# Turning layer 1's projection weights on VectorE instead of TensorE, and the masks of the first three steps on ScalarE

## The chip, the cores and the metric

The kernel runs on one core of a Trainium2 chip. The metric is device time in microseconds for one execution of the whole program; lower is better. The median of three runs before the change is 3088.62 us (3087.75 to 3088.84). Times "at" a point count from the start of the profiled span. Engines are PE (TensorE), DVE (VectorE), ACT (ScalarE), POOL (GpSimd) and SP, which only issues DMAs here; ACT issues DMAs too.

## The reference

64 graphs of 256 nodes with 512 features go through two attention layers. Layer 0 has 4 heads of 64, layer 1 has 8. All is float32.

```python
# layer 0
h = relu(layernorm(x))
q, k, v = h @ Wq, h @ Wk, h @ Wv                    # 512 -> 256
attn = softmax(where(adj, q k^T / 8, -max))
x = x + (attn v) @ Wo + bo
# layer 1
h = relu(layernorm(x))
h = layernorm(h) * gamma + beta
q, k, v = split(h @ w_qkv.T)                        # w_qkv is (1536, 512)
attn = softmax(where(adj | eye, q k^T / 8, -1e9))
x = x + (attn v) @ w_out.T + b_out                  # w_out is (512, 512)
```

Layer 1's weights come as (output, input). A matmul on PE contracts over the partitions, so the input feature has to lie on partitions: these weights have to be turned once.

## The kernel before

The work goes in 32 steps of two graphs each (512 tokens). In a step, tokens are split in 4 tiles of 128; the 512 features are split in 4 chunks (`c`) of 128 partitions. Everything is unrolled; nothing loops on the chip.

Each projection is done as a Strassen-like scheme of seven products (`PRODUCT`, `weight_sum`, `act_sums0`, `act_sums1`): a weight tile has 7 blocks, of which 4 are loaded; four sums (`weight_sum`, L404) make the other 3 and rewrite one of the 4, once. The activation tile `hT` has 7 blocks too, of which 4 are written from PSUM or placed by ACT, and four sums are made on POOL in every step (lines 407 to 412). A set of seven products for q and k is 28 matmuls (L841); the values of layer 0 use L888 in the turned form and L871 in the first two steps, those of layer 1 L922; the output projection L938, or L964 by rows in the first step. `evacuate` (L775 to L787) takes a product out of PSUM: products 1 and 2 by ACT copies, the others by DVE additions. Products 2, 4 and 3 go to the PSUM bank that 1, 7 and 5 had used, so product 3 waits for the evacuation of 5, and 4 for that of 7. The order in a set is 1, 6, 5, 2, 7, 3, 4; product 6 reads the activation sum `b[4]`, the second of POOL's sums (L410).

Attention of two heads is a "unit": scores on PE (L994), the mask added on DVE (L1017), exponentials on ACT (L1022), sums over halves of the keys on POOL (`pd`, L1029), turned and reduced on DVE (L1035, L1042, L1095 to L1107), sent through DRAM (`line`) and read back as the inverse sums (L1123), with which POOL normalises the result (L1141). `qk` of layer 0 is multiplied by the neighbour flags on POOL (L851).

The order on PE, DVE, ACT and POOL is written out by hand: `at(period, place, fn)` puts every piece at a place on a line, the pieces are sorted by it, and each engine gets its instructions in that order. A period (`PERIOD`, 6.4 places) is one step; negative periods are the start-up. Each engine works its own queue in order. SP is not in the list of hand-ordered engines, so the order of its DMAs follows from the build.

For the start-up before the change:

- `weight_load(n)` (L455 to L463) loads 4 x 128 rows of `w_qkv` (n = 0, 1, 2 for q, k, v) or of `w_out` (n = 3), one DMA of 1 MB each, into a buffer `wr` that is borrowed from another tile.
- `weight_block(wr, n, c)` (L465 to L473) turns one feature chunk `c`: four PE transposes (L468) into a PSUM bank, then two copies into the weight tile (L473), both on ACT for most q, k and v blocks, one on DVE and one on ACT for the first and for w_out. There are 16 such blocks, put between PE's pieces of steps 0 and 1.
- `weight_sum` for layer 1: q's on DVE (L404), the others on POOL.
- `mask(s, n)` (L544 to L551) makes the additive mask of a step from the adjacency on POOL (L549), 128 x 1024: 0 where there is an edge, -1e30 else. `mask0` then multiplies by the flags (L602), `mask1` by a tile that clears the diagonal (L610).
- `norm1` (L662 to L673) takes statistics of x on DVE and writes `h` = Relu(x - mean) on ACT (L673); `norm1_rest` takes h's statistics.
- In steps 0, 1 and the last, h is turned by PE; in the others by DVE in 32 x 32 blocks (`turn_blocks`, L724) with 16 DMAs (`move_blocks`, L736) that put the blocks in place, and ACT writes `hT` (`place_h`, L747, L749).

Of the kernel before, what the change touches and what calls it, by code (L numbers as in the profile page):

```python
# [18 lines left out]
LIMIT = 1e20  # L19


@with_exitstack
# [293 lines left out]
def fast_path(  # L316
# [61 lines left out]
    nc.vector.memset(extremes, 0.0)  # L378
    mhalf = const.tile([P, NT], FP, name="mhalf")
    nc.gpsimd.memset(mhalf, -0.5)  # L380

# [7 lines left out]

    Q, NQ = 32, P // 32
    NB = 7
    MARK = 64.0
# [20 lines left out]
    H0, H1, HD = I0 // 2, I1 // 2, D // 2  # L415
# [10 lines left out]
    def first_weights():  # L426
        for i in range(2):
            for k, w in enumerate((wq, wk)):
                nc.sync.dma_start(
                    wqk0[:, 2 * i:2 * i + 2, :, k, :].rearrange("p j c o -> p (j c) o"),  # L430
                    w[:, i * H0:(i + 1) * H0].rearrange("(c p) o -> p c o", p=P),
                )
        for i in range(2):
            nc.sync.dma_start(
                wv0[:, 2 * i:2 * i + 2].rearrange("p j c o -> p (j c) o"),
                wv[:, i * P:(i + 1) * P].rearrange("(c p) o -> p c o", p=P),
            )
# [8 lines left out]
        nc.scalar.dma_start(gbr[:NC], gamma.rearrange("(c p) -> c p", p=P))  # L446
        nc.scalar.dma_start(gbr[NC:], beta.rearrange("(c p) -> c p", p=P))
        return gbr

    def gamma_beta(gbr):  # L450
# [3 lines left out]

    def weight_load(n):  # L455

        if n == 1:
            wr = io.tile([P, 4, D], FP, name="wr", tag="xt")
        else:
            wr = act.tile([P, 4, D], FP, name="wr", tag="v1")  # L460
        src, r0 = (w_qkv, 4 * n) if n < 3 else (w_out, 0)
        nc.sync.dma_start(wr, src[r0 * P:(r0 + 4) * P].rearrange("(r p) i -> p r i", p=P))
        return wr  # L463

    def weight_block(wr, n, c):  # L465
        pw = mm_tile([P, 4 * P])
        for r in range(4):
            nc.tensor.transpose(pw[:, r * P:(r + 1) * P], wr[:, r, c * P:(c + 1) * P], ident)  # L468
        for i in range(2):
            blk = A_OF[i, c // HC]  # L470
            dst = wqkv1[:, blk, c % HC, n, :] if n < 3 else wo1[:, blk, c % HC, :]
            copy = nc.vector.tensor_copy if i == 0 and (n > 2 or (n, c) == (0, 0)) else nc.scalar.copy
            copy(dst, pw[:, i * H1:(i + 1) * H1])  # L473


    S = [dict() for _ in range(NSTEP)]
# [66 lines left out]

    def mask(s, n):  # L544
        if s < 2:
            edges, one = flat.bitcast(BF).rearrange("p (k c i) -> p k c i", k=NIC, i=P), 1.0
        else:
            edges, one = both[:, 1].rearrange("p k i t -> p k t i"), 1.0 + MARK
        nc.gpsimd.tensor_scalar(  # L549
            n.rearrange("p k g (c i) -> p k (g c) i", i=P), edges, -one, BIG, op0=ALU.add, op1=ALU.mult  # L550
        )  # L551

    def neighbours(s, g):

# [40 lines left out]
    def mask0(s):  # L595
# [4 lines left out]
        for kc in range(NIC):  # L600
            v = n0[:, kc].rearrange("p g n -> p (g n)")
            nc.gpsimd.tensor_tensor(v, v, st["ne"], ALU.mult)  # L602

    def mask1(s):
        st = S[s]
        n1 = st["n1"] = act.tile([P, NIC, G, N], BF, name="n1", bufs=2)
        mask(s, n1)
# [56 lines left out]
    def norm1(s, k):  # L664
        st, x1, t = S[s], S[s]["xt"], NORM1[k]
        if k == 0:
            st["mv"] = stat.tile([P, NT, 3], FP, name="mv1", bufs=2)
            st["mean"] = stat.tile([P, NT, 2], FP, name="mg", bufs=2)
            st["h"] = act.tile([P, NT, D], FP, name="h", tag="h" if s == NSTEP - 1 else "turned")
        mv, h = st["mv"], st["h"]  # L670
        moments(mv, x1, t)
        nc.scalar.mul(mv[:, t, 2:3], mv[:, t, 0:1], -1.0)
        nc.scalar.activation(h[:, t, :], x1[:, t, :], AF.Relu, bias=mv[:, t, 2:3])  # L673

    def second_bias(s, t):
        x1 = S[s]["xt"]
# [474 lines left out]
    def at(period, place, fn, *args):  # L1151
        events.append((period * (PERIOD if period >= 0 else FIRST) + place, len(events), fn, args))
# [77 lines left out]
    p = NSTEP - 2  # L1230
# [15 lines left out]
    for s in range(NSTEP):  # L1246
# [34 lines left out]
            at(p, place, adjacency_turn, s, a)  # L1281
        at(p, (FIRST_Q0 + 0.3, 3.74, 1.9)[s] if s < 3 else 3.58, mask0, s)
        at(p, (FIRST_Q0 + 0.31, 4.153)[s] if s < 2 else 5.85, mask1, s)
        if s == 0:
            at(p, FIRST_C0, first_transposes)
        else:
            for c in range(NC):
                if by_tensor(s, 0):
                    at(p, 2.9292 + 0.0001 * c, transpose_h, s, 0, c)
                else:  # L1290
                    at(p, AT_Q0 - 0.001 + 0.0001 * c, place_h, s, 0, c)
# [156 lines left out]
```

## Time and profile before

| | |
|---|---|
| median of 3 runs | 3088.62 us |
| the profiled execution | 3089.27 us, of which the span is 3087.4 us |
| granted PE clock | 1.00 |
| PE busy | 3068.8 us, 99% |
| DVE busy | 2539.7 us, 82% |
| POOL busy | 2308.9 us, 75% |
| ACT busy | 1207.4 us, 39% |
| DMA | 251.22 MB, mean 81 GB/s |

A line of the page's groups or of a timeline names the source line, the engine, the operation and the tiles, out<-in, then the number of instructions. In a timeline the first column is the start, the second the length of the merged stretch, and a bracket gives the idle time just before it and what ended it. PE's float32 matmuls appear as two records each, so a set of 28 shows x56. Matmuls overlap, and the end of each is modelled, so starts are the better measure on PE.

### The profile page before, as it was taken

To read this page: it belongs to the slowest core of one execution; us is meant where nothing else is said; L and a number is where in the kernel's file an instruction comes from. 1 tells how busy PE (TensorE), PEld (TensorE's weight loads), DVE (VectorE), ACT (ScalarE), POOL (GpSimd) and SP (SyncE) were. 2 spreads that over 40 slices of the span, in tenths; PEclk is the share of its full clock that TensorE was granted. 3 is DMA by queue.
4 is the path that set the end of the run, shared out by engine and by line. 5 is a ranking of instruction groups with operands and counts; after the bars stand their busy time and mean duration, and the time that the engine had idled before them with its cause. 6 is when DMAs were issued, how large, how long until landed. Compare 5 with 4: busy or idle time off the path is not lost.

```text
span 3087.4 us, 55474 instructions
## 1 busy us (share of the span) xinstructions
PE 3068.8 (99%) x20122; PEld 2528.5 (82%) x20122; DVE 2539.7 (82%) x4754; ACT 1207.4 (39%) x2136; POOL 2308.9 (75%) x2128
## 2 busy tenths in 40 slices
PE   8999999999999999999999999999999999999998
PEld 6878888888888888888888888888888888888887
DVE  7878888888888888888888888888888888888766
ACT  4434343344434343443434333443434344343431
POOL 7877877787877778777777778787777877777753
PEclk9999999999999999999999999999999999999999
DMA  4133232332322322223323233232332222331311
GB/s 152 53 95 92 57 90 74 93 94 64 86 74 87 94 84 70 84 73 100 93 55 92 72 93 94 67 83 73 87 94 87 68 84 75 99 93 52 93 34 50
DMA packets 187591, 251.22 MB, mean 81 GB/s; under 512 B 58088, under 2 KB 78192, under 8 KB 187312
## 3 DMA queue, kind: packets, MB, share of 16 engines
q1 hardware_dynamic: 123776, 179.93, 20.4%
q10 hardware_dynamic: 63536, 67.68, 7.6%
q8 instruction: 162, 2.65, 0.4%
q14 instruction: 117, 0.96, 0.1%
HBM read 128.59 MB, written 34.34 MB: 53 GB/s over the span
## 4 chain that ended last, share of the span: by engine, by line
PE 97%; POOL 2%; DVE 1%; issue 0%; DMA 0%; ACT 0%; ACTq 0%; SPq 0%; POOLq 0%; DVEq 0%
PE mm L841 37%; PE mm L938 18%; PE mm L922 13%; PE sc L994 9%; PE sc L1065 6%; PE mm L888 6%; PE mm L1065 5%; PE mm L994 3%; PE mm L871 1%; PE mm L964 0%; POOL pd L1029 0%; PE mm L468 0%; PE mm L700 0%; POOL xt L809 0%; POOL wqk L677 0%
## 5 line engine op out<-in xcount | busy, mean ns | idle before, releaser
L841 PE MATMUL mm<-hT,wqkv 128*128 128x256 f32 x3584 | 789.1, 380 | 1.9 <-DVE qk L779 0.9
L841 PEld LDWEIGHTS mm<-hT,wqkv 128*128 128x128 f32 x3584 | 677.3, 190 | 105.6 <-issue 11.8
L1029 POOL TENSOR_TENSOR pd<-p 128x512 f32<-128x512 f32 x383 | 479.6, 1274 | 257.5 <-ACT p L1022 199.6
L938 PE MATMUL mm<-wo,oT 128*128 128x256 f32 x2632 | 578.5, 379 | 0.0
L938 PEld LDWEIGHTS mm<-wo,oT 128*128 128x128 f32 x2632 | 499.8, 190 | 68.9 <-issue 0.7
L1022 ACT ACTIVATE p<-p 128x512 f32<-128x512 f32 x766 | 440.7, 626 | 119.3 <-DVE p L1017 109.1
L1017 DVE TENSOR_TENSOR p<-sc,n 128x512 f32<-128x512 f32 x579 | 362.6, 681 | 113.8 <-PE sc L994 113.6
L841 PE MATMUL mm<-hT,wqk 128*128 128x256 f32 x1792 | 398.7, 382 | 0.2
L922 PE MATMUL mm<-wqkv,hT 128*128 128x256 f32 x1792 | 395.5, 381 | 0.4 <-ACT v L775 0.4
L841 PEld LDWEIGHTS mm<-hT,wqk 128*128 128x128 f32 x1792 | 338.3, 191 | 55.8 <-issue 10.3
L922 PEld LDWEIGHTS mm<-wqkv,hT 128*128 128x128 f32 x1792 | 337.8, 190 | 55.7 <-issue 10.3
L809 POOL TENSOR_TENSOR xt<-xt,u 128x512 f32<-128x512 f32 x183 | 233.1, 1274 | 140.1 <-DVE xt L803 67.5
L994 PE MATMUL sc<-qk 64*128 64x256 f32 x2320 | 293.3, 385 | 1.0 <-DVE p L1017 1.0
L994 PEld LDWEIGHTS sc<-qk 64*128 64x128 f32 x2320 | 217.8, 186 | 61.5 <-issue 27.6
L1035 DVE STREAM_TRANSPOSE turned_p<-pd 128x1024 f32<-128x1024 f32 x192 | 237.1, 1235 | 32.2 <-POOL pd L1029 32.2
L631 ACT ACTIVATE h<-h,mr,r 128x512 f32<-128x512 f32 x252 | 187.8, 804 | 171.7 <-POOL mr L627 171.7
L1141 POOL TENSOR_TENSOR oT<-oT 128x512 f32<-128x512 f32 x188 | 240.3, 1278 | 0.6 <-DMA oT<-line 0.6
L1042 DVE TENSOR_REDUCE part<-turned_p 128x32 f32<-128x1024 f32 x192 | 233.1, 1214 | 4.4
L1065 PE MATMUL sc<-p,v 128*32 128x256 f32 x3152 | 190.8, 382 | 0.0
L888 PE MATMUL mm<-hT,wv 128*128 128x256 f32 x840 | 188.5, 382 | 0.3 <-ACT vT L775 0.3
L794 ACT COPY u<-mm 128x512 f32<-128x512 f32 x62 | 36.3, 586 | 368.6 <-PE mm L938 223.6
L888 PEld LDWEIGHTS mm<-hT,wv 128*128 128x128 f32 x840 | 156.6, 190 | 27.3 <-ACT vT L775 6.6
(154 smaller groups left out, 4439.0 us busy)
## 6 DMA issues: line engine op xcount, KB each, us to landing
h<-blocks SPq DMA_DIRECT2D x960, 64.0 KB, 2.0
oT<-line SPq DMA_DIRECT2D x376, 128.0 KB, 3.1
h<-in_x_dram SPq DMA_DIRECT2D x31, 1024.0 KB, 10.0
xt<-in_x_dram ACTq DMA_DIRECT2D x60, 512.0 KB, 4.3
out_dram<-xt SPq DMA_DIRECT2D x31, 512.0 KB, 3.1
out_dram<-xt ACTq DMA_DIRECT2D x31, 512.0 KB, 4.5
v<-values ACTq DMA_DIRECT2D x480, 32.0 KB, 1.9
ne<-ne SPq DMA_DIRECT2D x90, 64.0 KB, 2.0
```

Source lines behind the costliest of these rows:

```text
L809: (nc.vector if last else nc.gpsimd).tensor_tensor(r, r, u, ALU.add)
L841: nc.tensor.matmul(bank[:, k, :], w[:, wa, c, k, a * P:(a + 1) * P], st["hT"][:, ba, c, :], start=first and (k, c) == (0, 0), stop=(k, c) ...
L888: nc.tensor.matmul(bank, wv0[:, wa, c, :], st["hT"][:, ba, c, :], start=first and c == 0, stop=c == HC - 1, skip_group_check=True,)
L922: nc.tensor.matmul(bank[:, t, :], st["hT"][:, ba, c, t * P:(t + 1) * P], wqkv1[:, wa, c, 2, :], start=first and (t, c) == (0, 0), stop=(t, ...
L938: nc.tensor.matmul(bank[:, t, :], oT[:, ba, c, t * P:(t + 1) * P], w[:, wa, c, :], start=first and (t, c) == (0, 0), stop=(t, c) == (NIC - ...
L994: nc.tensor.matmul(sc[g][e][:, kc, :], qk[rows, 1, k0:k0 + P], qk[rows, 0, g * N:(g + 1) * N], start=True, stop=True,)
L1017: nc.vector.tensor_tensor(p[e][:, g], sc[e], neg[:, :, g, :], ALU.add)
L1022: nc.scalar.activation(p[e][:, g], p[e][:, g], AF.Exp, scale=SCALE)
L1029: nc.gpsimd.tensor_tensor(st["pd"][:, e], p[e][:, :, 0, :], p[e][:, :, 1, :], ALU.add)
L1035: nc.vector.transpose(st["turned_p"], st.pop("pd").rearrange("p e g (b k) -> p (e g b) k", k=32))
L1065: nc.tensor.matmul(po[r0:r0 + 32, g, :], (st["v1"][:, g * NIC + kc, pr * P + r0:pr * P + r0 + Q] if lyr else st["v0"][:, r0 // Q, pr, g * ...
L1141: nc.gpsimd.tensor_tensor(dst, dst, invb, ALU.mult)
```

## The change

Four things change in `fast_path`.

First, q, k and v of layer 1 are no longer turned by PE. `weight_load` loads each in four DMAs, one for each group of 32 partitions: group `b` holds, on its partition `p`, the rows `r*32 + p` and the 128 input features `b*128` to `b*128 + 127`. `weight_turn` then turns one chunk with one DVE instruction, which transposes blocks of 32 x 32 within each group. So partition `b*32 + n` of chunk `c` now holds feature `b*128 + c*32 + n`. w_out is still turned by `weight_block` on PE, now with both copies on ACT and in the four earliest places.

Second, the input features of layer 1 take this order everywhere: `norm1` writes `h` with the features reordered, and gamma and beta are loaded in that order.

Third, the masks of steps 0, 1 and 2 (both of each) are made by ACT as Identity(FAR * edges - FAR) with FAR = 2^100 in place of 1e30; the later ones stay on POOL with FAR. `mask1` is split in `mask1_fill` and the clearing of the diagonal.

Fourth, the order changes: the loads go q, k, w_out, v, all in the period of step 0's start; on SP the adjacency of step 2, which stood ahead of the first `line`, now comes after it; one of q's weight sums comes earlier, and two of w_out's weight sums on POOL go from step 0 to step 1.

```diff
-    def weight_block(wr, n, c):
+        pool, tag = ((act, "v1"), (io, "xt"), (act, "v1"), (act, "turned"))[n]
+        wr = pool.tile([P, 4, D], FP, name="wr", tag=tag)
+        if n == 3:
+            nc.sync.dma_start(wr, w_out.rearrange("(r p) i -> p r i", p=P))
+        else:
+            for b in range(NQ):
+                nc.sync.dma_start(
+                    wr[b * Q:(b + 1) * Q].rearrange("p r i -> p (r i)").rearrange("p (r i) -> p r i", i=P),
+                    w_qkv[n * D:(n + 1) * D, b * P:(b + 1) * P].rearrange("(r p) i -> p r i", p=Q),
+                )
         return wr
 
+    def weight_turn(wr, n, c):
+
+        j = c // HC
+        nc.vector.transpose(
+            wqkv1[:, j:j + 3:2, c % HC, n, :].rearrange("p i (r o) -> p i r o", o=Q),
+            wr.rearrange("p r i -> p (r i)").rearrange("p (i r c o) -> p c i r o", i=2, c=NC, o=Q)[:, c],
+        )
+
+    def weight_block(wr, c):
         pw = mm_tile([P, 4 * P])
         for r in range(4):
             nc.tensor.transpose(pw[:, r * P:(r + 1) * P], wr[:, r, c * P:(c + 1) * P], ident)
         for i in range(2):
-            blk = A_OF[i, c // HC]
-            dst = wqkv1[:, blk, c % HC, n, :] if n < 3 else wo1[:, blk, c % HC, :]
-            copy = nc.vector.tensor_copy if i == 0 and (n > 2 or (n, c) == (0, 0)) else nc.scalar.copy
-            copy(dst, pw[:, i * H1:(i + 1) * H1])
+            nc.scalar.copy(wo1[:, A_OF[i, c // HC], c % HC, :], pw[:, i * H1:(i + 1) * H1])
...
-        nc.gpsimd.tensor_scalar(
-            n.rearrange("p k g (c i) -> p k (g c) i", i=P), edges, -one, BIG, op0=ALU.add, op1=ALU.mult
-        )
+            edges = both[:, 1].rearrange("p k i t -> p k t i")
+        dst = n.rearrange("p k g (c i) -> p k (g c) i", i=P)
+        if s < 3:
+            nc.scalar.activation(dst, edges, AF.Identity, bias=far[:, s // 2:s // 2 + 1], scale=FAR)
+        else:
+            nc.gpsimd.tensor_scalar(dst, edges, -1.0 - MARK, FAR, op0=ALU.add, op1=ALU.mult)
...
-        nc.scalar.activation(h[:, t, :], x1[:, t, :], AF.Relu, bias=mv[:, t, 2:3])
+        nc.scalar.activation(
+            h[:, t, :].rearrange("p (c b n) -> p c b n", c=NC, b=NQ),
+            x1[:, t, :].rearrange("p (b c n) -> p c b n", c=NC, b=NQ), AF.Relu, bias=mv[:, t, 2:3],
+        )
...
+        at(p, (FIRST_Q0 + 0.305, 3.75, 5.45)[s] if s < 3 else 5.8499, mask1_fill, s)
...
-    for n, (p, place) in enumerate(((-2, 4.0), (-2, 4.0), (-1, 0.0), (-1, 1.1))):
-        at(p, place, lambda n=n: blocks.update({n: weight_load(n)}))
+    for n, place in ((0, 4.0), (1, 4.0), (3, 4.0), (2, 5.0)):
+        at(-2, place, lambda n=n: blocks.update({n: weight_load(n)}))
...
-    for i in range(16):
-
+    for i in range(12):
         place = (
-            *(3.3 - 3.93 + (1 + k) / 7 - 0.0005 for k in range(7)), 0.5205,
-            *(0.53 + 0.14 * (k + 1) - 0.0005 for k in range(4)), *(FIRST + (2 + k) / 7 - 0.0005 for k in range(4)),
+            4.6395, 4.6396, 4.9, 4.901, 4.902, 5.19965, 5.19966, 5.7, 12.6, 12.601, 12.602, 13.0,
         )[i]
-        at(-1, place, lambda i=i: weight_block(blocks[i // 4], i // 4, i % 4))
+        at(-2, place, lambda i=i: weight_turn(blocks[i // 4], i // 4, i % 4))
+    for c in range(4):
+        at(-1, 3.3 - 3.93 + (1 + c) / 7 - 0.0005, lambda c=c: weight_block(blocks[3], c))
     for i in range(4):
-        at(-1, 0.41 if i > 2 else 0.1 + 0.01 * i, weight_sum, nc.vector, wqkv1[:, :, :, 0, :], i)
+        at(-1, (-0.49, 0.1, 0.11, 0.41)[i], weight_sum, nc.vector, wqkv1[:, :, :, 0, :], i)
...
-        at(0, (4.7, 4.701, 4.702, 5.55)[i], weight_sum, nc.gpsimd, wo1, i)
+        at(*((0, 4.7), (0, 4.701), (1, 0.78), (1, 0.781))[i], weight_sum, nc.gpsimd, wo1, i)
```

By the order of the built program, PE loses 48 transposes; DVE gains 12 stream transposes and loses 5 copies; ACT loses 19 copies and gains 6 activations; POOL loses 6 mask instructions; SP issues 13 weight DMAs where it issued 4. PE's other instructions keep their order. The twelve transposes stand on DVE as follows: two before the mask of the first unit, three after the small copy of gamma and beta, two and one around the mask of the second unit, and v's four behind the second mask of step 1's layer 0: three at once, one ahead of the evacuation of product 7 in step 0's first layer-1 set.

More of the change, by code (lines that the diff above doesn't have):

```diff
@@ L19 @@
 LIMIT = 1e20
+FAR = 2.0 ** 100
+MARK = 64.0
 @with_exitstack
@@ L380, in fast_path @@
     nc.gpsimd.memset(mhalf, -0.5)
+    far = const.tile([P, 2], FP, name="far")
+    for i, one in enumerate((1.0, 1.0 + MARK)):
+        nc.gpsimd.memset(far[:, i:i + 1], -one * FAR)
     Q, NQ = 32, P // 32
     NB = 7
-    MARK = 64.0
     A_OF = {(0, 0): 0, (0, 1): 1, (1, 0): 2, (1, 1): 3}
@@ L445, in first_weights @@
         gbr = sm.tile([2 * NC, P], FP, name="gbr", tag="turned_p", bufs=1)
-        nc.scalar.dma_start(gbr[:NC], gamma.rearrange("(c p) -> c p", p=P))
-        nc.scalar.dma_start(gbr[NC:], beta.rearrange("(c p) -> c p", p=P))
+        for i, v in enumerate((gamma, beta)):
+            nc.scalar.dma_start(
+                gbr[i * NC:(i + 1) * NC].rearrange("c (b n) -> c b n", n=Q), v.rearrange("(b c n) -> c b n", c=NC, n=Q)
+            )
         return gbr
@@ L455, in weight_load @@
     def weight_load(n):
-        if n == 1:
-            wr = io.tile([P, 4, D], FP, name="wr", tag="xt")
-        else:
-            wr = act.tile([P, 4, D], FP, name="wr", tag="v1")
-        src, r0 = (w_qkv, 4 * n) if n < 3 else (w_out, 0)
-        nc.sync.dma_start(wr, src[r0 * P:(r0 + 4) * P].rearrange("(r p) i -> p r i", p=P))
-        return wr
-    def weight_block(wr, n, c):
+        pool, tag = ((act, "v1"), (io, "xt"), (act, "v1"), (act, "turned"))[n]
+        wr = pool.tile([P, 4, D], FP, name="wr", tag=tag)
+        if n == 3:
+            nc.sync.dma_start(wr, w_out.rearrange("(r p) i -> p r i", p=P))
+        else:
+            for b in range(NQ):
[3 more added lines that the diff above has]
+                )
+        return wr
+    def weight_turn(wr, n, c):
[5 more added lines that the diff above has]
+    def weight_block(wr, c):
         pw = mm_tile([P, 4 * P])
@@ L545, in mask @@
         if s < 2:
-            edges, one = flat.bitcast(BF).rearrange("p (k c i) -> p k c i", k=NIC, i=P), 1.0
+            edges = flat.bitcast(BF).rearrange("p (k c i) -> p k c i", k=NIC, i=P)
         else:
-            edges, one = both[:, 1].rearrange("p k i t -> p k t i"), 1.0 + MARK
-        nc.gpsimd.tensor_scalar(
-            n.rearrange("p k g (c i) -> p k (g c) i", i=P), edges, -one, BIG, op0=ALU.add, op1=ALU.mult
-        )
+            edges = both[:, 1].rearrange("p k i t -> p k t i")
[4 more added lines that the diff above has]
+            nc.gpsimd.tensor_scalar(dst, edges, -1.0 - MARK, FAR, op0=ALU.add, op1=ALU.mult)
     def neighbours(s, g):
@@ L602, in mask0, with mask1_fill @@
             nc.gpsimd.tensor_tensor(v, v, st["ne"], ALU.mult)
+    def mask1_fill(s):
+        n1 = S[s]["n1"] = act.tile([P, NIC, G, N], BF, name="n1", bufs=2)
+        mask(s, n1)
     def mask1(s):
-        st = S[s]
-        n1 = st["n1"] = act.tile([P, NIC, G, N], BF, name="n1", bufs=2)
-        mask(s, n1)
+        n1 = S[s]["n1"]
         for kc in range(NIC):
@@ L672, in norm1 @@
         nc.scalar.mul(mv[:, t, 2:3], mv[:, t, 0:1], -1.0)
-        nc.scalar.activation(h[:, t, :], x1[:, t, :], AF.Relu, bias=mv[:, t, 2:3])
+        nc.scalar.activation(
+            h[:, t, :].rearrange("p (c b n) -> p c b n", c=NC, b=NQ),
+            x1[:, t, :].rearrange("p (b c n) -> p c b n", c=NC, b=NQ), AF.Relu, bias=mv[:, t, 2:3],
+        )
     def second_bias(s, t):
```

## The prediction

> **What bounds the kernel now.** I read the page's busy shares first, then PE's waits over the whole run, then PE's timeline of the first 200 us and of one late step, and last POOL's, DVE's and ACT's timelines beside them.
>
> ```profile
> PE 3068.8 (99%) x20122; PEld 2528.5 (82%) x20122; DVE 2539.7 (82%) x4754; ACT 1207.4 (39%) x2136; POOL 2308.9 (75%) x2128
> ```
>
> PE is the bound. Its listed waits are 7.9 us for the first h, 2.2 us between 150 and 200 us, 1.4 us at the very end, and none from 200 to 3000 us. So only the first steps can change the time, unless the steady part gets slower. There PE's order is (start, length, engine, line):
>
> ```profile
> 55.62 0.60 PE L468 MATMUL mm<-ident,wr 128*128 128x128 f32 x4
> 56.05 1.89 PE L841 MATMUL mm<-hT,wqk 128*128 128x256 f32 x8
> 57.78 0.60 PE L468 MATMUL mm<-ident,wr 128*128 128x128 f32 x4
> 58.22 1.89 PE L841 MATMUL mm<-hT,wqk 128*128 128x256 f32 x8
> ```
>
> Starts, not lengths, tell the price, since the lengths contain a modelled tail: a weight block (four transposes) moves the next matmul by 0.44 us (57.78 to 58.22). Further on, in step 0:
>
> ```profile
> 157.23 2.75 PE L888 MATMUL mm<-hT,wv 128*128 128x256 f32 x12
> 160.27 3.72 PE L888 MATMUL mm<-hT,wv 128*128 128x256 f32 x16 [0.29 <-ACT vT L775]
> ...
> 171.17 1.99 PE L841 MATMUL mm<-hT,wqkv 128*128 128x256 f32 x8
> 173.50 7.17 PE L841 MATMUL mm<-hT,wqkv 128*128 128x256 f32 x32 [0.34 <-POOL hT L410]
> 181.53 1.99 PE L841 MATMUL mm<-hT,wqkv 128*128 128x256 f32 x8 [0.86 <-DVE qk L779]
> 184.26 1.97 PE L841 MATMUL mm<-hT,wqkv 128*128 128x256 f32 x8 [0.73 <-DVE qk L781]
> 186.06 12.25 PE L938 MATMUL mm<-wo,oT 128*128 128x256 f32 x56
> ```
>
> ```profile
> 1204.80 6.28 PE L888 MATMUL mm<-hT,wv 128*128 128x256 f32 x28
> 1211.01 1.93 PE L1065 MATMUL sc<-p,v 128*32 128x256 f32 x32
> ...
> 1218.25 12.35 PE L841 MATMUL mm<-hT,wqkv 128*128 128x256 f32 x56
> 1230.44 4.91 PE L938 MATMUL mm<-wo,oT 128*128 128x256 f32 x22
> ```
>
> The same L841 set takes 14.89 us in step 0 (171.17 to 186.06) and 12.19 later (1218.25 to 1230.44): 2.70 us of stalls. The L888 set takes 6.69 us (157.23 to PE's L1065 at 163.92) against 6.21: 0.48 us. The named releasers are DVE and ACT, but DVE waits there for POOL's pd (2.1 us before 178.38), and POOL runs without a gap from 145.3 on, because of work that no later step has:
>
> ```profile
> 147.77 3.99 POOL L404 TENSOR_TENSOR wo<-wo 128x512 f32<-128x512 f32 x3
> 162.11 1.29 POOL L404 TENSOR_TENSOR wo<-wo 128x512 f32<-128x512 f32 x1
> 168.42 1.05 POOL L549 TENSOR_SCALAR n<-both 128x1024 bf16<-128x1024 uint8 x1
> ```
>
> [...] In the trace, 512-byte rows (wqk, wv) with others give 298 GB/s (8 to 12 us), 2 KB rows 387 (21 to 24 us): near, not equal.
>
> **The change, part by part.**
>
> *Blocks off PE.* Of 16 blocks four remain (wo1's), in the places of the first four. Eight go between 57.78 and 73.34: 15.56 us become eight pieces of matmuls at 1.73, or about 13.8, so 8 x 0.436 = 3.49 us. Four more between 89.65 and 96.58: 1.74. Sum 5.23 us, all on PE's path.
>
> *Twelve transposes on DVE*, 128x512 each. The nearest row is L724, the same size in pieces of 32: four in 2.48 us, so 0.62 to 0.65 each. Places: two after the evacuation that ends at 28.98, before the mask at 30.68 (ends 30.3); three after the copy at 33.73, before turned_p at 36.04 (35.7); two from 42.17, before the mask at 43.61 (43.5); one from 46.09, with a weight sum (0.69) pulled forward, before the evacuation at 48.63 (47.4). All are covered by idle time of DVE that waits for PE or POOL. The last four (v) stand between 85 and 93 us, where DVE is full; below.
>
> *Loads.* q, k, wo1, v are issued earlier, 12 pieces of 256 KB in 512-byte rows. Before, the two megabytes of wr end at 27.0 and so start at about 21.6 (2.7 us each at 387 GB/s). From 21.6 at 290 GB/s (4 to 12 us) q lands at about 25.2, k 28.8, wo1 31.5. DVE needs q by 29.4, k by 35.0, PE needs wo1 by 46.2: cost nothing. Slow bound: at half that rate, should a 32-partition target halve it, q lands at 28.8 and k at 36.0: one microsecond on DVE, with no wait of PE. v's pieces wait for the last q transpose (34.9) and are issued by 38, ahead of the line at 41.96, h at 42.48 and adjacency, so these keep their times.
>
> *Masks on ACT.* 1.13 us each; bounds 1.0 (the L529 copy, 1024 wide) and 1.3. The first pair fills the gap of ACT from 19.98 to 31.40. The second pair stands at 54.8 to 57.1 ahead of the qk copy (55.82 before, now 57.1), whose readers on PE come at 61.2: hidden. POOL's product waits for it and starts at 55.95 instead of 56.13. The last two are in idle stretches of ACT. Relief of POOL: six times 1.05 to 1.36.
>
> *Order of features.* The Relu L673 reads in runs of 32. L747, which reads such runs, takes 0.55 us for 512, so no more than the 0.59 of a copy: zero. Cover: at 1277.4 the last Relu ends, at 1279.79 DVE needs it; 2.37 us. The small gamma and beta loads: zero.
>
> *What is late next.* PE reaches the scores that began at 80.34 at 76.85, 3.49 us ahead, but DVE is not. Its chain xt add, statistics, statistics of h costs 2.33 us a tile (71.21 to 73.54), and PE now delivers a tile every 1.72. Worked from the second tile at 66.6, the fourth xt add starts at 71.28 instead of 73.54. So DVE gains 2.26 here, and 2.46 at the masks (81.51 to 79.05), since a wait of 0.3 for PE goes. Its hT tiles (83.91) end by 82.97; POOL's sums follow as before (84.85 and 86.21, second end 87.49), now ending at 85.05. PE wants the second sum at 84.4 (82.68 + 1.73): a new stall of 0.65 us. Bounds 0.3 and 1.2. After it the four v transposes (2.5 us, less four wo copies at 0.41) load DVE: its evacuation of set 7 ends at about 93.7, PE wants that at 93.75. I take 0.1, bounds 0 and 0.8. DVE is even with PE again at 100.3.
>
> *Stalls of step 0.* POOL loses two weight sums (2.56 us) and a mask (1.05) by 170, more than the 2.70 + 0.48. Laid out anew, pd starts 1.6 us after the L841 set (4.7 before, 1.2 in the later step), and DVE's turned_p follows the evacuation at once, as in the later step. I take 3.15; bounds 2.0 and 3.2. The two sums moved to step 1 (2.56) lie in POOL's gap of 4.19 before 192.71's counterpart.
>
> *Sum.* -5.23 + 0.65 + 0.1 - 3.15 = -7.63 us. The profiled execution took 3089.27 with a span of 3087.4; it becomes 3081.6 and 3079.8. It stood 0.65 above the median, so the median goes from 3088.62 to 3081.0.
>
> **The rivals.**
>
> 1. *The lead is lost on the way*: DVE's and POOL's waits around 84 to 100 us and in step 0 keep most of their length, because a faster PE only meets them sooner. For: DVE is over 80% busy there, and two of my margins are under 0.3 us. Against: POOL's relief is larger than the stall. With the upper bounds of the new stalls (1.2 + 0.8) and half of the recovery (1.6): -5.23 + 2.0 - 1.6 = -4.8, so 3083.8.
> 2. *No new stall at 84 us*: -5.23 - 3.18 = -8.4, so 3080.2. It needs DVE's chain to tighten; nothing shows how.
> 3. *Late weights park DVE* (slower): the k transpose stands ahead of turned_p at 36.04. If k lands at L, DVE is late by L - 35.0, less 1.6 of idle up to the evacuation that PE waits for at 49.3, and PE stalls for the rest. It cancels the gain from L = 44.2, that is if both megabytes after h1 (21.6) move at under 93 GB/s. The only 32-partition pieces in the trace, h<-blocks, run 16 x 64 KB in 10.04 us (104 GB/s), though paced by their issue. At 80 GB/s k lands at 47.8 and the stall is 11.2: 3092.2. Against: 512-byte rows moved at 290.
>
> **How the numbers follow.** A measurement of this kernel tells about 0.2% (6.2 us) from no change. Chances: main case 0.55 (3080 to 3082.4), rival 2 0.08, rival 1 0.27 (within 0.2% for most of its span), rival 3 or another slowdown 0.10, half of that within 0.2%. Faster 0.62 (main, rival 2, little else), same 0.32, slower 0.06. The range reaches from rival 2's end, 3079.6, through rival 1's, with its worst bounds and a recovery of 0.5: 3088.6 - 3.7 = 3084.9; I take 3085.5.
>
> **What would show it.** Right: no L468 on PE after 56; the matmuls from 56.05 to the L871 set without gaps; a PE wait for POOL's hT near 84; L841 in step 0 in 12.2 us; wr transposes at 0.62 to 0.65 with no DMA wait ahead. Wrong: DVE waiting for wr; PE waits for DVE at 93 or 100; POOL still without a gap at 165; a Relu over 0.72 or any PE wait between 200 and 2900 us.

## The result and the profile after

The changed kernel takes 3080.75 us (median; 3080.05 to 3084.99), the kernel before 3088.61 beside it: a ratio of 0.9976, 95% interval 0.9969 to 0.9984, or 7.86 us less. Forecast: 3081.0, 7.6 less. The profiled execution took 3080.29 us with a span of 3078.5 (before: 3089.27 and 3087.4).

The page of the changed kernel, busy time, share of the span and instructions of each engine:

```profile
PE 3062.4 (99%) x20074; PEld 2524.2 (82%) x20074; DVE 2546.2 (83%) x4761; ACT 1207.7 (39%) x2123; POOL 2299.7 (75%) x2124
```

PE executes 48 matmuls fewer and is still the bound. PE's timeline (start, length, engine, line), where twelve weight blocks used to stand and then the first layer-1 set:

```profile
39.76 1.93 PE L1087 MATMUL sc<-p,v 128*32 128x256 f32 x32
...
55.24 5.35 PE L863 MATMUL mm<-hT,wqk 128*128 128x256 f32 x24
...
76.01 2.00 PE L1016 MATMUL sc<-qk 64*128 64x256 f32 x16
...
81.82 1.99 PE L863 MATMUL mm<-hT,wqkv 128*128 128x256 f32 x8
84.25 10.72 PE L863 MATMUL mm<-hT,wqkv 128*128 128x256 f32 x48 [0.43 <-POOL hT L414]
94.89 1.93 PE L1087 MATMUL sc<-p,v 128*32 128x256 f32 x32
...
158.20 1.93 PE L1087 MATMUL sc<-p,v 128*32 128x256 f32 x32
...
165.44 12.35 PE L863 MATMUL mm<-hT,wqkv 128*128 128x256 f32 x56
177.63 12.25 PE L960 MATMUL mm<-wo,oT 128*128 128x256 f32 x56
```

The same places in the kernel before:

```profile
40.58 1.93 PE L1065 MATMUL sc<-p,v 128*32 128x256 f32 x32
...
80.34 2.00 PE L994 MATMUL sc<-qk 64*128 64x256 f32 x16
...
86.09 3.72 PE L841 MATMUL mm<-hT,wqkv 128*128 128x256 f32 x16
```

No weight transposition is left after 55; the 24 matmuls at 55.24 run in one piece. The scores come at 76.01 instead of 80.34. Product 6 of the first layer-1 set waits for POOL's second sum (L414, the old L410): the one new wait in this stretch. In step 0 the set takes 177.63 - 165.44 = 12.19 us instead of 14.89.

POOL's timeline in step 0, where three weight sums, a fourth and a mask had stood:

```profile
142.49 2.64 POOL L408 TENSOR_TENSOR wo<-wo 128x512 f32<-128x512 f32 x2
...
171.25 2.50 POOL L1051 TENSOR_TENSOR pd<-p 128x512 f32<-128x512 f32 x2 [0.78 <-DVE turned_p L1057]
...
180.00 2.60 POOL L408 TENSOR_TENSOR wo<-wo 128x512 f32<-128x512 f32 x2
184.21 0.20 POOL L667 TENSOR_SCALAR ve<-mv 128x4 f32<-128x4 f32 x1 [1.61 <-DVE mv L635]
```

POOL now waits for DVE at 171 instead of being late, and the two moved sums end before a gap of 1.61 us. What the prediction had held only as its slow bound stands in DVE's timeline and in the load rate (columns of the windows: stretch, its length, busy us of PE, PEld, DVE, ACT, POOL, granted PE clock, DMA share, GB/s):

```profile
34.95 0.71 DVE L478 STREAM_TRANSPOSE wqkv<-wr 128x512 f32<-128x512 f32 x1 [0.83 <-DMA wr<-in_L_gnn_w_qkv_dram]
...
39.15 0.73 DVE L599 TENSOR_SCALAR rows<-identb,any_of 128x128 bf16<-128x128 bf16 x4
```

```profile
24.00:26.00 2.00, 2.00 (x11) 1.76 (x10) 1.75 (x5) 0.00 (x0) 0.00 (x0) 1.00 1.23 190
```

The weights arrive at 190 GB/s, k at 34.9 us. DVE waits 0.83 us for it, and 4.2 us later four small instructions (L599) end at 39.88, while POOL's sums start at 39.72. In this execution that cost PE nothing. In others it did, as the runs below show.

### The profile page after: what moved, and what is told of

Same layout as the page of the kernel before. It is cut to its first block, busy times and chain, and to the rows that moved or that the text cites. A ratio compares the mean times of both kernels' runs of the same rounds, so it can differ in the third digit from the quotient of the medians.

```text
span 3078.5 us, 55362 instructions
## 1 busy us (share of the span) xinstructions
PE 3062.4 (99%) x20074; PEld 2524.2 (82%) x20074; DVE 2546.2 (83%) x4761; ACT 1207.7 (39%) x2123; POOL 2299.7 (75%) x2124
## 4 chain that ended last, share of the span: by engine, by line
PE 98%; DVE 1%; POOL 0%; DMA 0%; ACT 0%; issue 0%; SPq 0%; ACTq 0%; DVEq 0%; POOLq 0%
PE mm L863 38%; PE mm L960 18%; PE mm L944 13%; PE sc L1016 9%; PE sc L1087 6%; PE mm L910 6%; PE mm L1087 5%; PE mm L1016 3%; PE mm L893 0%; PE mm L986 0%; DVE bs L634 0%; POOL wqk L699 0%; DMA h<-in_x_dram 0%; POOL xt L831 0%; PE mm L722 0%; DVE p L1039 0%
## 5 line engine op out<-in xcount | busy, mean ns | idle before, releaser
L863 PE MATMUL mm<-hT,wqkv 128*128 128x256 f32 x3584 | 787.8, 380 | 0.4 <-POOL hT L414 0.4
L863 PEld LDWEIGHTS mm<-hT,wqkv 128*128 128x128 f32 x3584 | 677.8, 190 | 103.5 <-issue 11.6
L863 PE MATMUL mm<-hT,wqk 128*128 128x256 f32 x1792 | 398.1, 382 | 0.3 <-ACT qk L797 0.2
L863 PEld LDWEIGHTS mm<-hT,wqk 128*128 128x128 f32 x1792 | 338.5, 191 | 56.0 <-issue 10.3
L1016 PE MATMUL sc<-qk 64*128 64x256 f32 x2320 | 293.4, 385 | 1.0 <-DVE p L1039 1.0
L1016 PEld LDWEIGHTS sc<-qk 64*128 64x128 f32 x2320 | 218.0, 186 | 61.3 <-issue 27.2
L1087 PE MATMUL sc<-p,v 128*32 128x256 f32 x3152 | 190.8, 382 | 0.0
L910 PE MATMUL mm<-hT,wv 128*128 128x256 f32 x840 | 188.3, 382 | 0.0
L910 PEld LDWEIGHTS mm<-hT,wv 128*128 128x128 f32 x840 | 156.7, 190 | 26.8 <-ACT vT L797 6.2
```

The source lines that it names most:

```text
L863: nc.tensor.matmul(bank[:, k, :], w[:, wa, c, k, a * P:(a + 1) * P], st["hT"][:, ba, c, :], start=first and (k, c) == (0, 0), stop=(k, c) ...
L910: nc.tensor.matmul(bank, wv0[:, wa, c, :], st["hT"][:, ba, c, :], start=first and c == 0, stop=c == HC - 1, skip_group_check=True,)
L1016: nc.tensor.matmul(sc[g][e][:, kc, :], qk[rows, 1, k0:k0 + P], qk[rows, 0, g * N:(g + 1) * N], start=True, stop=True,)
L1087: nc.tensor.matmul(po[r0:r0 + 32, g, :], (st["v1"][:, g * NIC + kc, pr * P + r0:pr * P + r0 + Q] if lyr else st["v0"][:, r0 // Q, pr, g * ...
```

## The experiments

Theory A, the prediction's: the gain is the twelve blocks off PE (5.2), less a new stall near 84 us, plus the stalls of step 0, which are POOL's doing. Theory B: PE's blocks are nearly all of it, and what POOL and ScalarE do is not on the path. The expectation of each run says what A and B mean for it.

All times, with the ratio to the kernel before on the same chip:

| run | median us | lowest to highest | ratio, 95% |
|---|---|---|---|
| e1 masks on POOL | 3086.24 | 3082.22 to 3087.56 | 0.9988 (0.9980 to 0.9996) |
| e2 sums in step 0 | 3083.93 | 3081.47 to 3088.15 | 0.9987 (0.9980 to 0.9993) |
| e3 weights alone | 3088.28 | 3084.94 to 3092.55 | 1.0000 (0.9991 to 1.0008) |
| e4 POOL relief alone | 3085.71 | 3085.07 to 3086.88 | 0.9991 (0.9983 to 0.9999) |
| c0 changed kernel again | 3081.27 | 3079.76 to 3082.43 | 0.9976 (0.9967 to 0.9986) |
| e8 (the same, see there) | 3080.66 | 3079.88 to 3084.67 | 0.9977 (0.9968 to 0.9986) |
| e5 less on DVE at 84 | 3080.30 | 3079.46 to 3081.69 | 0.9974 (0.9964 to 0.9984) |
| e7 k later | 3085.60 | 3083.44 to 3087.30 | 0.9990 (0.9982 to 0.9998) |
| e6 loads to 128 partitions | 3079.87 | 3079.14 to 3080.64 | 0.9972 (0.9960 to 0.9983) |
| e9 k behind the keys | 3080.72 | 3079.62 to 3082.15 | 0.9974 (0.9964 to 0.9983) |
| e10 masks on POOL, h first | 3087.39 | 3081.78 to 3090.37 | 0.9994 (0.9986 to 1.0002) |
| e12 three easings | 3085.35 | 3080.29 to 3088.08 | 0.9986 (0.9980 to 0.9993) |

Many of these scatter over 3 to 9 us, where the kernel before keeps within about 3. So each was read from one profile by stretches of PE's timeline, from the start of one group to the start of another (us):

| | A: first L863 to L1087 | B: L540 to the L863 after it | C: L1016 to L863 | D: first layer-1 set | E: L910, step 0 | F: L863, step 0 |
|---|---|---|---|---|---|---|
| before | 28.16 | 1.01 | 5.75 | 14.04 | 6.69 | 14.89 |
| after | 27.89 | 1.01 | 5.81 | 13.07 | 6.21 | 12.19 |
| e1 | 32.18 | 1.01 | 7.27 | 12.30 | 6.21 | 12.76 |
| e2 | 28.36 | 1.01 | 5.81 | 13.07 | 6.65 | 13.66 |
| e3 | 27.52 | 2.89 | 9.62 | 12.28 | 6.70 | 14.90 |
| e4 | 28.24 | 1.01 | 5.75 | 14.04 | 6.21 | 12.19 |
| c0 | 27.43 | 2.90 | 5.80 | 13.08 | 6.21 | 12.19 |
| e5 | 27.92 | 1.02 | 5.75 | 12.90 | 6.20 | 12.19 |
| e6 | 27.39 | 1.01 | 5.81 | 13.08 | 6.21 | 12.19 |
| e7 | 29.25 | 4.08 | 5.81 | 13.07 | 6.21 | 12.19 |
| e8 | 27.37 | 1.73 | 5.80 | 13.06 | 6.21 | 12.19 |
| e9 | 27.83 | 1.01 | 5.81 | 13.07 | 6.21 | 12.19 |
| e10 | 27.38 | 4.70 | 9.60 | 12.28 | 6.21 | 12.78 |
| e12 | 28.15 | 4.70 | 5.75 | 12.91 | 6.20 | 12.19 |

Undisturbed, a set of 56 is 12.19 and B 1.01. Where a single profile and a median differ, the table of stretches says what an edit does in its place, the medians what an execution costs as a rule. From the output projection of step 0 to the end, the profiled spans take 2900.8 to 2902.6 us (before: 2901.3); so up to 1.8 us between two profiles lie outside the stretches, and PE's list of waits doesn't explain them.

### The parts undone: e1 to e4

e1, the masks of steps 0 to 2 back on POOL:

```diff
-        if s < 3:
+        if s < 0:
             nc.scalar.activation(dst, edges, ...)
...
-        at(p, (FIRST_Q0 + 0.305, 3.75, 5.45)[s] if s < 3 else 5.8499, mask1_fill, s)
+        at(p, (FIRST_Q0 + 0.3099, 4.1529)[s] if s < 2 else 5.8499, mask1_fill, s)
```

> The changed kernel with the masks of steps 0 to 2 back on POOL, where they were. Theory A (POOL's load sets the stalls of the first step, and the second pair of masks on ScalarE lets POOL's product and its sums start in time): POOL makes the second pair of masks at 54 to 57 us and its products start later, so PE waits about 1.4 us for ScalarE at L722's counterpart near 78 us, but the 0.9 us stall at 84 us goes, because PE comes later; and about 0.7 us of stall comes back in the L863 set of step 0. Sum +1.2, median about 3082.0. Theory B (the masks on ScalarE cost or save nothing, all the gain is TensorE's twelve blocks and the two sums): no change within 0.3, 3080.7, with the stall at 84 us as it is.

The stretches are as theory A has them: C +1.46, D -0.77, F +0.57, together 1.26. But the times fall into two groups, six runs from 3082.22 to 3083.47 and seven from 3086.24 up; the lower is 0.9 above what was expected (3082.0), the upper was expected by neither theory. The profiled run was of the upper group, and its stretch A is 4.3 us too long. DVE's and PE's timelines there:

```profile
26.48 0.69 DVE L634 BATCH_NORM_STATS2 bs<-h 128x6 f32<-128x512 f32 x1 [3.62 <-DMA h<-in_x_dram]
```

```profile
28.11 3.07 PE L863 MATMUL mm<-hT,wqk 128*128 128x256 f32 x8 [2.53 <-DVE qk L803]
...
83.65 0.33 PE L722 MATMUL mm<-ident,h 128*128 128x128 f32 x1 [0.85 <-ACT h L650]
84.36 1.86 PE L722 MATMUL mm<-ident,h 128*128 128x128 f32 x15 [0.38 <-ACT h L650]
```

The h of step 1 landed 3.6 us after DVE wanted it. DVE ran nothing from 22.86 to 26.48, and the evacuation behind these statistics (L803) began at 27.31 instead of 23.55; PE waited 2.53 us for it. The windows of PE after that stall:

```profile
28.00:29.00 1.00, 0.89 (x4) 0.84 (x5) 0.96 (x3) 0.00 (x0) 0.00 (x0) 0.91 1.13 193
29.00:30.00 1.00, 1.00 (x4) 0.82 (x3) 0.96 (x3) 0.00 (x0) 0.57 (x1) 0.50 1.10 165
30.00:31.00 1.00, 1.00 (x4) 0.73 (x4) 0.93 (x3) 0.00 (x0) 0.70 (x1) 0.50 1.08 208
31.00:32.00 1.00, 1.00 (x4) 0.82 (x3) 0.73 (x2) 0.00 (x0) 0.86 (x2) 0.50 1.03 189
32.00:33.00 1.00, 1.00 (x6) 0.84 (x5) 1.00 (x2) 0.00 (x0) 0.85 (x4) 0.89 1.09 173
```

The granted clock is 0.50 from about 28.8 to 32.2 us: three whole windows, 0.18 us of the first (0.09 / 0.5) and 0.22 of the last, 3.4 us in all. So a stall of 2.53 us costs 4.2: itself, and half of the 3.4 us. Stretch A is 4.3 longer. (The eight matmuls at 28.11 take 3.07 us instead of 1.89.) Why h landed late in this run is open: it was issued at 12.43 us, 0.48 after the changed kernel's, and took 14.0 us instead of 10.6. At 83.65 the cost of these masks is seen, which the theory had named: ACT's h waits 2.22 us for mr, which POOL makes late after two masks (59.40 and 66.82, 1.04 each) in its queue.

e2, the last two wo1 sums back in step 0:

```diff
-        at(*((0, 4.7), (0, 4.701), (1, 0.78), (1, 0.781))[i], weight_sum, nc.gpsimd, wo1, i)
+        at(0, (4.7, 4.701, 4.702, 5.55)[i], weight_sum, nc.gpsimd, wo1, i)
```

> The changed kernel with the last two wo1 sums of POOL back in step 0, the masks left on ScalarE. Theory A (the recovery in step 0 comes from POOL's relief): some 2.1 to 2.4 us of stalls return between 150 and 190 us, 0.5 in the L910 set (6.7 instead of 6.21) and the rest in the L863 set (about 14 instead of 12.19), median about 3083.0. Theory B (the stalls went because PE, or DVE with its weights, comes there in another phase): both sets stay at 6.2 and 12.2, median about 3080.8.

PE's timeline of e2:

```profile
175.54 1.99 PE L863 MATMUL mm<-hT,wqkv 128*128 128x256 f32 x8 [0.23 <-DVE qk L801]
178.27 1.97 PE L863 MATMUL mm<-hT,wqkv 128*128 128x256 f32 x8 [0.74 <-DVE qk L803]
180.07 12.25 PE L960 MATMUL mm<-wo,oT 128*128 128x256 f32 x56
```

The stalls are back at the same two products: F +1.47, E +0.44; B, C and D are unchanged, A is 0.47 longer. Theory A, with 1.9 us (2.1 to 2.4 expected); the median is 3.2 above the changed kernel's, more than these two stretches explain; the rest is open.

e3 is e1's and e2's edits together.

> Both undone: masks and sums of POOL as before, so that only the turning of the weights by VectorE, their loads and the order of the features are left of the change. Theory A: the two stalls of step 0 return whole (3.2 us: L863 set 14.9, L910 set 6.7) and the wait near 78 us of the kernel with masks on POOL is there too (net +0.75); 3080.8 + 3.9 = about 3084.7, a gain over before of about 3.9. Theory B (lead is simply added, POOL matters little): about 3081 to 3082.

F and E are those of the kernel before to 0.01 us, as theory A said. But the median shows no gain, and is 3.6 above the expected one; only five runs of thirteen (3084.94 to 3086.06) come near. The profile (of 3089.6) has more than was expected in two places: B +1.88, where nothing was, and C +3.81, where e1 had 1.46. At C, PE's longest wait is 1.58 us instead of e1's 0.85, and behind it the granted clock is 0.50 from 82.3 to 85.7 us. Theory A's terms stand, and something is missing in it.

e4 is the kernel before with POOL's relief alone:

```diff
-        at(0, (4.7, 4.701, 4.702, 5.55)[i], weight_sum, nc.gpsimd, wo1, i)
+        at(*((0, 4.7), (0, 4.701), (1, 0.78), (1, 0.781))[i], weight_sum, nc.gpsimd, wo1, i)
...
+        if s == 2:
+            at(p, 5.45, mask1_fill, s)
```

> The kernel before with POOL's relief in step 0 alone: the two wo1 sums moved to step 1 and the first mask of step 2 on ScalarE; the sixteen weight blocks stay on TensorE, the loads and the order of features as before. Theory A: the stalls of step 0 go (L841 set 12.2, L888 set 6.2), gain 3.2, median about 3085.4. Theory B (these stalls come from the late start of PE's first layer-1 set, so POOL's relief alone can't lift them): 3088.6.

3085.71: PE's timeline has the set whole, and C and D as before:

```profile
170.39 12.35 PE L855 MATMUL mm<-hT,wqkv 128*128 128x256 f32 x56
182.58 9.66 PE L952 MATMUL mm<-wo,oT 128*128 128x256 f32 x44
```

So POOL's relief lifts the stalls of step 0 with PE's blocks still in place. The times keep within 1.8 us: the scatter comes with the rest of the change, the new loads and the weights on VectorE among it.

### The missing part: c0, e8, e7

c0 is the changed kernel once more.

> The changed kernel once more, as the measure for the three that run beside it. Theory A (the second chunk's h lands with no slack, and in some executions after DVE needs it, which stalls TensorE for about 2.5 us and then halves its granted clock for some 3.4 us): most times at 3080.5, a part of them 3.5 to 4.5 us higher. Theory B (the high times of the earlier variants come of their own edits): all within 3080 to 3082.

The times scatter, but without a group 4 us up; the profiled run (3081.98) shows why. Its DVE, POOL and PE timelines:

```profile
35.11 0.71 DVE L478 STREAM_TRANSPOSE wqkv<-wr 128x512 f32<-128x512 f32 x1 [1.38 <-DMA wr<-in_L_gnn_w_qkv_dram]
...
39.31 2.79 DVE L599 TENSOR_SCALAR rows<-identb,any_of 128x128 bf16<-128x128 bf16 x4
```

```profile
39.33 1.37 POOL L411 TENSOR_TENSOR hT<-hT 128x512 f32<-128x512 f32 x1 [4.20 <-ACT hT L726]
40.78 1.27 POOL L414 TENSOR_TENSOR hT<-hT 128x512 f32<-128x512 f32 x1
```

```profile
49.19 0.66 PE L486 MATMUL mm<-ident,wr 128*128 128x128 f32 x4 [1.42 <-ACT wo L488]
50.06 1.99 PE L863 MATMUL mm<-hT,wqk 128*128 128x256 f32 x8 [0.22 <-DVE qk L799]
```

DVE is only 0.16 us later at 35.11 than in the profile shown first, and POOL 0.39 earlier, because PE had turned h 0.39 earlier (L722 at 37.53 instead of 37.92). With that the four L599 instructions meet POOL's sums and take 2.79 us instead of 0.73; they end at 42.10, where POOL's second sum ends (42.05). From there the delay runs down DVE's masking, ACT's exponentials and ACT's copy of wo to PE's second weight block: B +1.89. Over all profiles that lengthening and PE's wait at L486 go together:

| | after, e1, e2, e5, e6, e9 | e8 | c0 | e3 | e7 | e10 | e12 |
|---|---|---|---|---|---|---|---|
| four L599, us | 0.73 | 1.77 | 2.79 | 2.79 | 3.13 | 3.24 | 3.78 |
| PE waits at L486, us | 0 | 0.23 | 1.42 | 1.41 | 2.57 | 3.22 | 3.22 |

In every long case L599 starts after, or less than 0.2 us ahead of, POOL's first sum; in the profiles of after, e1, e2 and e5 it starts 0.57 to 0.89 us ahead. The four take 0.25 us each in the changed kernel's profile, where only the last of them lies beside a sum, for 0.16 us. In five of the six long cases L599 ends within 0.06 us of the end of a POOL sum (c0: 42.10 and 42.05); in e8, 0.22 after it. So the lengthening comes where L599 stands beside POOL's sums, and most often ends with one of them; by what means one holds up the other, no run shows.

e8 was to load the h of step 1 ahead of xt:

```diff
-            at(p, (0.0, 0.2)[edge], load_x, s)
+            at(*((-2, 3.25), (p, 0.2))[edge], load_x, s)
```

> The changed kernel with the second chunk's h and adjacency loaded ahead of the residual xt of step 0, which is first read at 48 us. h lands some 2.7 us earlier, near 20 us instead of 22.5. Theory A: DVE never waits for h, the high times of part of the executions go, all within about 3080 to 3081.5, median 3080.5 or lower. Theory B (h is not the cause of the spread): times scatter as with the changed kernel.

This edit doesn't change that order: in SP's timeline xt (10.74) still goes ahead of h (12.05). h has one buffer, its load stands where PE has read the h of step 0 (PE's last transposition of it ends at 11.91), and SP's order isn't that of the program's places. So e8 is a third measurement of the changed kernel: two of twelve runs are at 3083.8 and 3084.7, the profiled one has B +0.72.

e7, w_out ahead of q and k:

```diff
-    for n, place in ((0, 4.0), (1, 4.0), (3, 4.0), (2, 5.0)):
+    for n, place in ((3, 4.0), (0, 4.0), (1, 4.0), (2, 5.0)):
```

> The changed kernel with w_out's megabyte loaded ahead of q's and k's, so that q and k land about 3 us later (k at 37.7 instead of 34.9). It prices a late weight on DVE. Theory A (DVE is in order, so each us by which k is late beyond its idle time of 1.6 us up to L799 reaches TensorE): DVE's wait for wr rises from 0.8 to about 3.5 us, TensorE stalls about 2.1 us near 48 us, median 2 to 3 above the changed kernel, about 3083; more, if the stall also lowers the granted clock. Theory B (the wait is taken up by idle time of DVE further on): no change, 3080.7.

Theory A's direction, at almost twice its price: 4.3 above c0. DVE waits 3.94 us for q and 0.57 for k (q is late as well, at 32.2, which the expectation had not thought through). The masking behind q's turning begins at 33.42, although PE's scores for it had ended at 30.72; L599 then takes 3.13, and PE loses 3.07 at B, with a clock of 0.50 from 52.2 to 55.6 us, and about 1.4 in A.

### The levers: e5, e6, e9, e10, e12

e5, for the stall at 84 us:

```diff
-            4.6395, 4.6396, 4.9, 4.901, 4.902, 5.19965, 5.19966, 5.7, 12.6, 12.601, 12.602, 13.0,
+            4.6395, 4.6396, 4.9, 4.901, 4.902, 5.19965, 5.19966, 5.7, 6.282, 6.568, 12.602, 13.0,
...
-            place = (-5.0, -4.999, -4.998, 0.29)[a] if s == 2 else ...
+            place = (-5.0, -4.999, 0.289, 0.29)[a] if s == 2 else ...
```

> The changed kernel with less of DVE's work between 77 and 92 us: v's first two transposes moved to about 56 and 60 us, and one pair of the adjacency transposes of step 2 moved behind the second masking. Theory A (the new 0.88 us stall at 84 us hangs on DVE's hT tiles, behind which POOL's sums stand): DVE reaches the hT tiles about 0.7 us earlier, the stall falls to 0.2 or less, median 0.6 to 0.9 below the changed kernel, about 3080.0. Theory B (POOL's own queue sets the stall): as the changed kernel, 3080.7.

PE's timeline:

```profile
81.57 10.63 PE L863 MATMUL mm<-hT,wqkv 128*128 128x256 f32 x48
92.58 1.97 PE L863 MATMUL mm<-hT,wqkv 128*128 128x256 f32 x8 [0.38 <-DVE qk L803]
94.47 1.93 PE L1087 MATMUL sc<-p,v 128*32 128x256 f32 x32
```

The stall at 84 is gone: DVE's work ahead of its hT tiles was its cause (theory A). In its place product 4 waits at 92 for the evacuation of product 7, behind turned_p and a weight transposition: the set takes 12.90 instead of 13.07, a gain of 0.17 and not 0.6 to 0.9. The median, 3080.30, is the lowest of the versions that compute the whole, but from c0 and e8 beside it (3081.27 and 3080.66) it can't be told with certainty.

e6 loads the pieces to all partitions, which leaves the weights of layer 1 in a wrong order:

```diff
-                    wr[b * Q:(b + 1) * Q].rearrange("p r i -> p (r i)").rearrange("p (r i) -> p r i", i=P),
-                    w_qkv[n * D:(n + 1) * D, b * P:(b + 1) * P].rearrange("(r p) i -> p r i", p=Q),
+                    wr[:, b].rearrange("p (r i) -> p r i", i=P),
+                    w_qkv[n * D:(n + 1) * D, b * P:(b + 1) * P].rearrange("(r p) i -> p r i", p=P),
```

> The changed kernel with q's, k's and v's pieces loaded to all 128 partitions instead of one group of 32, with the same 256 KB a piece and the same 512-byte rows. The weights of layer 1 then stand in a wrong order, so the output is not the reference's; number, shapes and places of all instructions stay. Theory A (a target of 32 partitions halves the rate): between 22 and 30 us the load runs at 290 to 390 GB/s instead of 190, k lands near 30 us instead of 35, DVE's wait for wr goes, and with it the spread that comes of it; median 0.2 to 0.8 below the changed kernel's. Theory B (rows of 512 bytes and not the 32 partitions set the rate): 190 GB/s and the times as before.

The windows of e6:

```profile
24.00:26.00 2.00, 2.00 (x12) 1.74 (x11) 1.73 (x4) 0.00 (x0) 0.54 (x1) 1.00 1.21 290
```

290 GB/s instead of 190 with the same rows: theory A, though 190 is two thirds of 290 and not the half. DVE has no wait for wr, L599 takes 0.73, and the seven runs keep within 1.5 us, the median 0.85 under e9's beside it. Rows of 2 KB to 128 partitions, in one DMA of 1 MB, had 387 in the kernel before; so the shorter rows or the smaller pieces, which no run separates, take their part (387 to 290), and the group of 32 partitions the rest. Why fewer partitions take less, no run shows.

e9 takes k's first turning out of the tight place:

```diff
-            4.6395, 4.6396, 4.9, 4.901, 4.902, 5.19965, 5.19966, 5.7, 12.6, 12.601, 12.602, 13.0,
+            4.6395, 4.6396, 4.9, 4.901, 5.19964, 5.19965, 5.19966, 5.7, 12.6, 12.601, 12.602, 13.0,
```

> The changed kernel with k's first turning moved on DVE from ahead of turned_p (35 us) to the two others at 41.6 us, where DVE waits for the second set of scores. Theory A (k lands at the moment that DVE wants it; a little later, and DVE's four small L599 instructions, 0.73 us in all, meet POOL's hT sums, take 1.8 to 2.8 us, and TensorE stalls up to 1.6 us near 48): DVE has no wait for wr there, L599 takes 0.73 us, no TensorE wait for wo at 48 us; the low end of the times stays near 3079.8 and the median comes down by 0.2 to 0.6, to about 3080.4. Theory B (L599's length has another cause): times and waits as the changed kernel.

In its profile all is as theory A has it: no wait for wr at 35, L599 at 38.65 in 0.73, B 1.01. The times (3079.62 to 3082.15) are no different from the changed kernel's. One profile that might have been good anyway, and a median that doesn't move: not decided.

e10 and e12 issue xt on ScalarE's queue, so that h goes sooner:

```diff
-            at(p, (0.0, 0.2)[edge], load_x, s)
+            at(*((-2, 3.96), (p, 0.2))[edge], load_x, s)
...
-        nc.sync.dma_start(xt, ...)
+        (nc.scalar if s == 0 else nc.sync).dma_start(xt, ...)
```

with e9's edit, e10 on top of e1, e12 on top of e5.

> The kernel with the masks back on POOL, whose times fell into two groups (3082.2 to 3083.5 and 3086.2 to 3087.6), with the residual xt of step 0 no longer ahead of the second chunk's h on SP but issued by ScalarE behind its first copies, and k's first turning moved to 41.6 us. h then lands some 1.4 us earlier. Theory A (the upper group is the second chunk's h landing after DVE needs it: a TensorE stall of 2.5 us and half the clock after it): the upper group goes, median about 3082.3, near the 3082.0 expected at first for the masks. Theory B (the groups come from the masks on POOL themselves): both groups stay, median over 3084.

> The changed kernel with all three easings: v's first two transposes and a pair of adjacency transposes away from 84 us, k's first turning at 41.6 us, and the residual xt behind the second chunk's h. Theory A (the stall at 84 us, the late k and the late h are separate and each costs what the traces show): median about 3079.8, none above 3081.5. Theory B (one easing makes the next wait late, or the xt issued later delays k and wo1): no lower than with the first alone, 3080.3, or higher.

Both got worse, as theory B has it, though in e10 not for its reason. xt, issued at 10.6 us in the changed kernel, goes out later. The DMAs move 319 and 297 GB/s from 22 to 26 us in e10, 299 and 306 from 24 to 28 in e12, where the changed kernel has 186 to 194: more than the weights' pieces is under way there, and that it is xt beside q is an estimate from these rates. In both profiles DVE waits for q (2.02 and 1.54 us) ahead of the first masking, and meets POOL with L599. e12's DVE and PE timelines:

```profile
39.70 3.78 DVE L599 TENSOR_SCALAR rows<-identb,any_of 128x128 bf16<-128x128 bf16 x4
```

```profile
51.22 0.66 PE L486 MATMUL mm<-ident,wr 128*128 128x128 f32 x4 [3.22 <-ACT wo L488]
```

16 of e12's 21 runs lie from 3084.28 up, 5 from 3080.29 to 3082.47. That settles what a late weight can do: 3.7 us at B, and in e12 the clock on top (0.50 from 53.0 to 56.4 us). It doesn't settle e1's upper group: h's wait fell to 0.63 in e10 and most runs were still high, but for another cause.

## Why the prediction was right, and where not

- *Blocks off PE*, -5.23: right. (Between 57.78 and 73.34 there are seven pieces of matmuls, about 12.1 us, and not eight with 13.8; the 3.49 that follows is right.) 80.34 became 76.01, 4.33 earlier, of which 0.82 came from an earlier start (L1087 at 39.76 instead of 40.58). So 3.51 for eight blocks (3.49 said). The set with the other four went from 14.04 to 13.07, which with its stall of 0.88 is 1.85 (1.74 said).
- *What is late next*, +0.65 +0.1: with 0.82 added for the start, DVE's fourth xt add came at 71.35 (71.28 said), the masks at 79.05 (79.05), the second sum ended at 85.01 (85.05). The stall is 0.70 at the named place, and 0.88 in the whole set. The 0.1 at 93.75 was nil as long as the first stall stood; e5 shows that it takes over when that goes. Rival 2 needed both to go.
- *Stalls of step 0*, -3.15: 0.48 + 2.70 = 3.18 by the timelines; e2 shows that POOL's two sums make 1.9 of it, e4 that it goes without the blocks' help, and e1 puts the masks' part at 0.57. Another 0.7 is lost only where both are undone (e3, 3.20).
- *Sum*: PE stands 8.43 ahead at 177.63; less the start, 7.61 (7.63 said). The start was not foreseen; 0.55 of it is there at the first L863 (11.87, before 12.42), ahead of every mask and weight. 40.29 with the old loads (e4) and 39.37 with the new (c0) both occur, and 40.29 with the new too (e2); whether the change makes it is open. The other 0.5 of the spans' difference (8.9) comes in later stretches, in no listed wait.
- *Loads*, "cost nothing": the step that failed, and DVE waiting for wr was one of the prediction's own signs of being wrong. The rate was taken from transfers to 128 partitions (290, which e6 confirms), and k was put at 28.8. It landed at 34.9, near the slow bound (36.0; its half of the rate was the author's guess, e6 shows two thirds), and that was said to cost "one microsecond on DVE, with no wait of PE". True in the profile first shown; in c0 and e8 PE lost 1.89 and 0.72 to it, since the sum held DVE's idle time against the delay and not what DVE would meet when late. That the median still lies 0.2 from the forecast is in part luck: the early start on one side and the late k on the other were both left out. What the late k costs the median isn't measured apart; e6, where it can't happen, lies 0.85 below e9 beside it.
- *Rival 3* had the right mechanism (e7: 3.94 us without work on DVE, and the masking behind it late) and too low a price: L - 35.0 less 1.6 of idle gives 1.1 us for e7's k at 37.7, and the kernel lost 4.3. It counted neither q, which was late too, nor L599, nor the clock.
- *Masks on ScalarE* were priced as a small help to POOL in step 0. Their instructions cost what was said (1.14 to 1.16 us; the 1.13 was the author's estimate, against 1.01 for the L529 copy of the same width), but e1 (C +1.46) and e3 (+3.81, with the clock) show that without them POOL's statistics would have come too late for a PE that is 3.5 us ahead. The prediction saw the second pair only as "hidden". It is one of the parts that keep the lead, rival 1, from being lost: e3, the weights alone, has a median no better than before, with the masks at C, the stalls of step 0 and a late k all against it.
- Small terms: transposes 0.66 to 0.71 (0.62 to 0.65 said), twelve times on no path; Relu 0.72 as before; between 215 and 2990 us PE waits for nothing.

## What to carry to other kernels

A lead gained on the bounding engine is kept only where its feeders have room: look at what each of them does in the stretch just after, and move that in the same change, since the parts don't add up (here nothing for the weights alone and 2.8 us for POOL's relief alone, 7.9 together with the masks of steps 0 and 1; these weren't run alone, but the first of these masks starts at 19.2 us in the kernel before, and from there to 157 us its list has no wait of PE that they could have shortened). When a new load or wait is put ahead of other work of an engine, ask not only whether idle time covers its delay but what that work will run beside when it comes later (L599 took 0.73 us in its place, 2.79 in c0). Where a kernel's times begin to scatter, profile it twice: the waits that differ name the transfer that has no slack.

## What the runs showed of the hardware

- Loads of 512-byte rows, in pieces of 256 KB, moved at 186 to 194 GB/s to one group of 32 partitions (changed kernel, 22 to 32 us), at 290 to 301 to all 128 (e6, 22 to 28 us).
- Four bf16 TENSOR_SCALARs of DVE (L599) took 0.73 us where they stood ahead of POOL's TENSOR_TENSORs (changed kernel, e1, e2, e5), and 1.77 (e8) to 3.78 (e12) beside them.
- At or just after PE waits of 1.6, 2.5, 2.6 and 3.2 us (e3, e1, e7, e12), the granted clock was 0.50 for 3.4 us each time, so that about 1.7 us came on top of the wait; after waits of 1.4 (c0) and 3.2 (e10, at 47 to 50 us) it stayed at 1.00. After a wait of 1.6 in e10 (at 82 us), 15 transpositions took 3.46 us where e12's 16 took 1.97; the clock there was not read. So the length of a wait alone didn't tell whether the clock went down.
